# One graph-convolution layer's two weight products done as seven products of halves, moved between the two attention pairs

## The chip, the cores and the metric

The kernel runs on one core of one Trainium2 chip, in one launch, on inputs and outputs in float32. The metric is the device time of the launch in microseconds (us): the median of three runs.

## What is computed

There are 16 independent examples, each a table of 1024 nodes by 256 channels, and one table of neighbours `adj` (1024 by 1024) that all share. Each example goes through two layers. The first is an attention of 4 heads whose queries come from a weighted neighbour sum; the second is a pair of graph convolutions. Both add their input and normalize. Cut to what matters:

```
# layer 0
g   = relu(einsum('bcn,bnm->bcm', x^T, adj * likeness(x)) * para)      # queries
k,v = x @ kv_w
x1  = layernorm(x + softmax(q k^T * scale) v)
# layer 1
h1  = relu(x1 @ w1_loop + adj @ (x1 @ w1_neigh) + b1)                  # 256 -> 128 channels
h2  = relu(h1 @ w2_loop + adj @ (h1 @ w2_neigh) + b2)                  # 128 -> 256 channels
out = layernorm(x1 + (x1 + h2) * 0.5)
```

In the program the weights are named `w1n` (neigh) and `w1l` (loop). The change is about `x1 @ w1_neigh` (called t1), `x1 @ w1_loop` (the loop term), and the statistics of the last layernorm ("LN2").

## The kernel before

The kernel is a software pipeline over the examples, written out by hand: each engine executes its instructions in the order in which `run()` (from L1265) emits them, and an instruction waits until its inputs are there and its output buffer is free. While iteration `b` does the attention of example b, it also does the first convolution of example b-1 (`c1`), the second convolution of example b-2 (`c2`), the last normalization of example b-3 (`c3`), and the queries, keys and values of example b+1. Iterations 2 to 14 take the branch from L1398, and iteration 15 takes the one at L1442 and L1519; those fourteen are the ones that the change touches. The first two iterations and the end after iteration 15 have code of their own.

One iteration of the steady state is, in TensorE's order:

1. `both_units(0)` (L774): scores (L715) and weighted values (L761) of the first pair of heads. A pair has two units of 512 queries; a unit has eight score tiles of 128 keys. `scores` puts a tile in a PSUM tile called "big" (two banks, three such tiles exist), or, for every fourth, in two single banks; ScalarE takes the exponential into an SBUF row tile (L720, L722); VectorE adds the eight exponentials (L734, L736), turns the sum (L743) and reduces it (L749). `outputs` then reads the exponentials again, and each one's row tile comes free after that read.
2. `both_units(1)`: the same for the second pair.
3. `c1.inner()` (L910): t1 of example b-1. Sixteen products of 128 by 128 by 128 with channel-major x1 as the stationary operand, so that t1 comes out with nodes on partitions; ScalarE copies it out (L918).
4. `Joined.run` (L1204): the neighbour sums of t1 (for example b-1) and of h1 (for b-2) together, as seven products of halves (L1201) against stored parts of `adj`. The loop term is accumulated by `c1.loop` (L922) straight into the same PSUM banks: columns 0 to 511 ahead of product 1, columns 512 to 1023 ahead of product 3. The h2 products (L1026) lie inside it.
5. The queries (L660) and the keys and values (L448, L452) of example b+1.

"Seven products of halves" is the scheme in which a product of two by two blocks takes seven block products and some additions in place of eight. The kernel used it already for the queries, keys and values, the neighbour sums, and h2.

A float32 product of 128 by 128 by 512 is two matmul instructions here. The trace's counts are instructions.

SBUF work space is mostly one ring of 31 row tiles (`row_tile`, L99) of 128 by 1024 floats. A new row takes the slot that came free longest ago, and its first writer waits for that slot's last reader. All data transfers are issued on SyncE's queue (SPq), in program order; a transfer that waits for a row holds up those behind it. `before_convolution` (L1406) issues the first parts of `adj` for `Joined.run` and two rows of `adj` for the queries. It is emitted after the scores of the second pair.

`Joined.left` (L1187) makes sums of t1 and h1 on GpSimd (L1192 to L1195), and `q.left` sums of x (L619 to L622), which overwrite the blocked copy of x that `channel_major` (L1418) has turned.

The LN2 statistics are `c3.moments()` (L1422): eight times bn_stats (L314) and bn_aggr (L315) on VectorE, then eps (L319) and GpSimd's power (L320). `finish_aside` (L1075) applies them on ScalarE.

A row tile, the transposition by VectorE (which turns 32 by 32 blocks) and a write to DRAM with a permuting pattern turn a whole table: `turn_blocks` (L941) and `load_h1` (L950) do this for h1 already.

Of the kernel before, what the change touches and what calls it, by code (L numbers as in the profile page):

```python
# [18 lines left out]
def kernel(  # L19
# [34 lines left out]
    P = 128  # L54
# [33 lines left out]
    def half_psum(name):  # L88
        return big_psum(name)[:, 0:FB]
# [40 lines left out]
    kv_sums = dram.tile([P, N], F32, tag="kv_sums", name="kv_sums", bufs=1)  # L130
    w2_sums = dram.tile([P, 5 * P], F32, tag="w2_sums", name="w2_sums", bufs=1)

    def sum_kv_weights():
# [11 lines left out]
    def load_weights():  # L145
        nc.sync.dma_start(out=w1l_sb, in_=w1_loop.rearrange("(cc p) f -> p cc f", p=P))
        nc.sync.dma_start(out=w1n_sb, in_=w1_neigh.rearrange("(cc p) f -> p cc f", p=P))
        nc.sync.dma_start(out=w2l_sb, in_=w2_loop)
        nc.sync.dma_start(out=w2n_sb, in_=w2_neigh)
        nc.sync.dma_start(out=b1_sb, in_=b1.rearrange("(p o) -> p o", o=1))  # L150
        nc.sync.dma_start(out=b2_sb, in_=b2.rearrange("(o f) -> o f", o=1).to_broadcast([P, C]))

        for w in (w2l_sb, w2n_sb, b2_sb):
            nc.gpsimd.tensor_scalar_mul(w, w, 1.0 / 3.0)
        for w in (w1l_sb, w1n_sb):
            nc.gpsimd.tensor_scalar_mul(w, w, LIFT)
# [8 lines left out]
        nc.sync.dma_start(out=w2_sums, in_=t[:, 0:5 * P])  # L165

    ident = const.tile([P, P], F32, name="ident")
# [519 lines left out]
    class Attention:  # L687
# [85 lines left out]

        def both_units(self, pair, first=lambda: None, second=lambda: None, third=lambda: None):  # L774
            u = NJ * pair
# [11 lines left out]
            self.collect(u + 1, 6, 7)  # L787
            accB = self.turned_sum(u + 1)
            self.outputs(u + 1, turned=False)
            nc.vector.transpose(row[:, FB:N], self.o.pop(u + 1))  # L790
            self.part_sum(u + 1, accB)
            third()
# [106 lines left out]
    class GraphConv:  # L899


        def __init__(self, b, xT, nodes=None, x=None):
            self.b, self.xT, self.nodes, self.x = b, xT, nodes, x
            self.w2 = None

# [4 lines left out]
        def inner(self):  # L910
# [6 lines left out]
            self.t1 = row_tile(f"t1_{b}").rearrange("p (t f) -> p t f", f=HID)  # L917
            nc.scalar.copy(self.t1, p1.rearrange("p (t f) -> p t f", f=HID))  # L918

        def loop(self, ph, j, start=False, again=False):  # L920
# [147 lines left out]
        def deviation(self):  # L1068
            self.rstd = reciprocal_deviation(self.mv, f"g{self.b}", EPS2)

        def finish(self, dst):
            normalize(self.mv, self.rstd, self.x)
            nc.sync.dma_start(out=dst.rearrange("(t p) c -> p t c", p=P), in_=self.x)

        def finish_aside(self, dst, halfway=lambda: None):  # L1075

            shift = small.tile([P, NT], F32, tag="shift", name=f"shift_{self.b}", bufs=1)
            nc.vector.scalar_tensor_tensor(shift, self.mv[:, :, 0], -1.0, self.rstd, op0=ALU.mult, op1=ALU.mult)
            for t in range(NT):
# [6 lines left out]
        def ending(self, dst, quarters, aside, filled):  # L1086
# [18 lines left out]
            def deviations(*tiles):  # L1105
# [7 lines left out]
                statistics(mv, rows, range(n), f"e{tiles[0]}")  # L1113
                (nc.vector if tiles == (NT - 1,) else nc.gpsimd).tensor_scalar_add(rstd, mv[:, :, 1], EPS2)
                nc.gpsimd.tensor_tensor(rstd, rstd, neg_half[:, 0:n], ALU.pow)
# [13 lines left out]
            half = FB // NJ  # L1129
            banks = {}  # L1130
# [12 lines left out]
            aside(lambda: nc.scalar.copy(self.uT[:, FB:FB + half], third[:, 0:half]))  # L1143
            products(0, 1)
# [16 lines left out]
            leave(*stats)  # L1161
            products(6)
            stats = deviations(6)
            leave(*stats)
            products(7)
            _, mv, rstd, _ = deviations(7)
            normalize(mv, rstd, self.x[:, 7:8, :], 1)
            nc.sync.dma_start(out=dst[7 * P:8 * P, :], in_=self.x[:, 7, :])

    class Joined:  # L1170
# [33 lines left out]
        def run(self, between=None, last=None):  # L1204
# [18 lines left out]
            self.product(2, third)  # L1223
            nc.vector.tensor_add(p1, p1, third)
# [40 lines left out]
    def run():  # L1265
# [59 lines left out]
        for b in range(B):  # L1325
# [72 lines left out]
            elif more:  # L1398
                nodes = None

                def sums():
                    nonlocal nodes
                    nodes = NodeSums(q, xb, str(b + 1))
                    c2.load_x()

                def before_convolution():  # L1406
# [22 lines left out]
                def more_weights():  # L1429
# [3 lines left out]
                    if c3:  # L1433
# [6 lines left out]
                         last=nc.gpsimd)  # L1440
                c1.turn_blocks()
            else:  # L1442
                att.both_units(0)
                att.both_units(1, third=lambda: att.add_pairs(0))
# [74 lines left out]
            else:  # L1519
                c2.load_x()  # L1520
                both.fetch("00", "10", 2, 3)
                c1.inner()
                both.left(nc.gpsimd)
# [95 lines left out]
```

## Time and profile before

| | |
|---|---|
| median of 3 runs | 2119.41 us (2119.29 to 2120.25) |
| the profiled execution | 2119.75 us |
| its span, first to last instruction | 2118.0 us |
| granted TensorE clock | 0.999 |
| busy: TensorE, VectorE, ScalarE, GpSimd | 2107.8, 1866.3, 1136.3, 338.8 us |
| one steady iteration | 130.31 us |
| moved by DMA | 346.38 MB, mean 164 GB/s |

The period is the distance of the same instruction in two iterations (the first scores begin at 1172.74 and at 1303.05). In the profile PE is TensorE's matmul, PEld its weight load, DVE VectorE, ACT ScalarE, POOL GpSimd, SPq SyncE's DMA queue. A matmul's shown duration includes its way through the pipeline, so the pace is read from the chain of waits, which lists consecutive work with start, duration and number of instructions.

### The profile page before, as it was taken

Reading aid. Unit: us, or ns where it says so; the run is one execution under the profiler, and the core shown is the slowest. Engines: PE = TensorE matmul, PEld = TensorE weight load, DVE = VectorE, ACT = ScalarE, POOL = GpSimd, SP = SyncE. Lnnn points to the kernel's source line nnn. Section 1 sums busy time; section 2 is a strip of 40 time slices with the busy share of each in tenths; the row PEclk is TensorE's granted clock in tenths of the full one; section 3 lists DMA queues with packets and bytes.
Section 4 is the critical chain, followed back from the end, with each engine's and each line's share of the span. In section 5 each row is a group of like instructions: output and inputs, shape, how many; then the busy total and the mean of one; then the engine's idle time right before and its main releaser. Section 6 shows DMA issues by size and latency. Waiting matters only on the chain.

```text
span 2118.0 us, 24985 instructions
## 1 busy us (share of the span) xinstructions
PE 2107.8 (100%) x8724; PEld 1034.4 (49%) x8724; DVE 1866.3 (88%) x2264; ACT 1136.3 (54%) x1673; POOL 338.8 (16%) x223
## 2 busy tenths in 40 slices
PE   9999999999999999999999999999999999999998
PEld 5344435445454454545545454454544535445355
DVE  6899998898898998888988889888898888898875
ACT  5845564546546465473654736447455474555523
POOL 2010102131021311203122031210312102131022
PEclk9999999999999999999999999999999999999999
DMA  9495764856639476384764749557385673955545
GB/s 221 113 181 190 141 184 141 157 181 130 209 106 192 175 137 221 109 166 175 144 217 118 162 169 169 195 127 171 146 178 187 145 177 125 190 177 132 176 131 176
DMA packets 613732, 346.38 MB, mean 164 GB/s; under 512 B 492000, under 2 KB 556896, under 8 KB 613600
## 3 DMA queue, kind: packets, MB, share of 16 engines
q1 hardware_dynamic: 613328, 344.45, 63.0%
q8 instruction: 71, 1.16, 0.2%
q14 instruction: 61, 0.50, 0.1%
q10 hardware_dynamic: 272, 0.26, 0.0%
HBM read 294.45 MB, written 50.20 MB: 163 GB/s over the span
## 4 chain that ended last, share of the span: by engine, by line
PE 99%; DVE 0%; POOL 0%; issue 0%; POOLq 0%; DVEq 0%
PE s L715 21%; PE av L761 21%; PE hu_ps L1201 17%; PE g_ps L660 16%; PE v_ps L452 5%; PE k_ps L448 5%; PE hu_ps L1026 4%; PE t_ps L915 3%; PE g_ps L579 3%; PE hu_ps L922 2%; PE u_ps L966 1%; PE h_ps L937 1%; PE h_ps L1026 1%; PE sum_ps L275 0%; PE idle L1275 0%; PE h_ps L922 0%
## 5 line engine op out<-in xcount | busy, mean ns | idle before, releaser
L736 DVE TENSOR_TENSOR acc<-acc,pr 128x1024 f32<-128x1024 f32 x384 | 481.2, 1253 | 34.6 <-DVE acc L736 0.5
L722 ACT ACTIVATE pr<-s 128x1024 f32<-128x1024 f32 x392 | 391.5, 1121 | 173.9 <-PE s L715 173.9
L715 PE MATMUL s<-qT,kT 64*128 64x512 f32 x2048 | 448.7, 592 | 0.0
L761 PE MATMUL av<-pr,v 128*64 128x512 f32 x2048 | 447.0, 594 | 0.0
L715 PEld LDWEIGHTS s<-qT,kT 64*128 64x128 f32 x2048 | 195.3, 187 | 241.7 <-issue 183.7
L761 PEld LDWEIGHTS av<-pr,v 128*64 128x64 f32 x2048 | 144.1, 137 | 297.3 <-issue 269.1
L1201 PE MATMUL hu_ps<-adj,R 128*128 128x512 f32 x480 | 213.6, 592 | 0.0
L365 POOL TENSOR_TENSOR rstd<-rstd,neg_half 128x32 f32<-128x32 f32 x16 | 88.3, 5520 | 625.3 <-DVE rstd L363 625.3
L1192 POOL TENSOR_TENSOR R<-h 128x512 f32<-128x512 f32 x14 | 29.6, 2116 | 810.0 <-DVE o L786 697.2
L571 DVE SCALAR_TENSOR_TENSOR wg<-wg,adj 128x1024 f32<-128x1024 f32 x128 | 150.2, 1212 | 3.6 <-ACT wg L566 3.6
L720 ACT ACTIVATE pr<-s 128x512 f32<-128x512 f32 x240 | 143.0, 708 | 0.0
L565 ACT ACTIVATE wg<-c_row,c_sums 128x1024 f32<-128x1024 f32 x120 | 139.7, 1164 | 2.1 <-DVE wg L571 0.9
L1201 PEld LDWEIGHTS hu_ps<-adj,R 128*128 128x128 f32 x480 | 89.0, 190 | 100.9 <-issue 100.7
L566 ACT ACTIVATE wg<-wg 128x1024 f32<-128x1024 f32 x128 | 135.4, 1057 | 4.1
L918 ACT COPY t<-t_ps 128x1024 f32<-128x1024 f32 x16 | 16.2, 1014 | 174.9 <-PE t_ps L915 174.9
L660 PE MATMUL g_ps<-wg,x 128*128 128x512 f32 x224 | 107.7, 593 | 0.0
L660 PE MATMUL g_ps<-T,xB 128*128 128x512 f32 x208 | 107.3, 597 | 0.0
L660 PE MATMUL g_ps<-wg,xB 128*128 128x512 f32 x208 | 106.2, 592 | 0.0
L1201 PE MATMUL hu_ps<-adj,t 128*128 128x512 f32 x240 | 105.7, 592 | 0.0
L734 DVE TENSOR_TENSOR acc<-pr,pr 128x1024 f32<-128x1024 f32 x64 | 77.9, 1217 | 22.4 <-ACT pr L722 22.4
L743 DVE STREAM_TRANSPOSE accB<-acc 128x1024 f32<-128x1024 f32 x64 | 79.7, 1245 | 2.2
L749 DVE TENSOR_REDUCE den_part<-accB 128x32 f32<-128x1024 f32 x64 | 76.9, 1201 | 1.2
(252 smaller groups left out, 3070.7 us busy)
## 6 DMA issues: line engine op xcount, KB each, us to landing
adj<-adjT SPq DMA_DIRECT2D x210, 512.0 KB
adj<-in_adj_dram SPq DMA_DIRECT2D x128, 512.0 KB
para<-in_L_gnn_para_dram SPq DMA_DIRECT2D x32, 512.0 KB
xB_a<-in_x_dram SPq DMA_DIRECT2D x128, 128.0 KB
x1d<-xB_a SPq DMA_DIRECT2D x128, 128.0 KB
x<-x1d SPq DMA_DIRECT2D x16, 1024.0 KB
xB<-in_x_dram SPq DMA_DIRECT2D x120, 128.0 KB
x<-in_x_dram SPq DMA_DIRECT2D x15, 1024.0 KB
```

The costliest lines, as they stand in the source:

```text
L448: nc.tensor.matmul(dst, self.a[0][n], self.w[n], start=not again, stop=True, skip_group_check=again)
L452: nc.tensor.matmul(dst[:, ts(t, P)], self.w[n][:, ts(t, P)], self.a[1][n], start=not again and t == 0, stop=True, skip_group_check=again o ...
L565: nc.scalar.activation(wg, self.c_row, AF.Abs, bias=self.c_col[:, t:t + 1], scale=-1.0)
L566: nc.scalar.activation(wg, wg, AF.Tanh, scale=-0.5 / C)
L571: nc.vector.scalar_tensor_tensor(wg, wg, 1.0, self.adj.pop(t), op0=ALU.add, op1=ALU.mult)
L660: nc.tensor.matmul(self.p[n], x_n[:, k, :], w_n, start=(k == 0), stop=(k == TJ - 1))
L715: nc.tensor.matmul(halves[s], self.kT[rows, pair, ts(mt, P)], self.qT[rows, pair, ts(j, FB)], start=True, stop=True)
L720: nc.scalar.activation(pr[:, ts(s, FB)], halves[s], AF.Exp)
L722: nc.scalar.activation(pr, ps, AF.Exp)
L736: nc.vector.tensor_add(self.acc, self.acc, prs[mt])
L761: nc.tensor.matmul(pav[s * HD:(s + 1) * HD, :], self.v[:, mt, pair * P + s * HD:pair * P + (s + 1) * HD], prs[mt][:, ts(s, FB)], start=(mt ...
L1201: nc.tensor.matmul(dst, self.x[n][:, k, :], of_rows(rows, k), start=(start and k == 0), stop=(k == TJ - 1), skip_group_check=again)
```

## The change

`c1.inner()` and both `c1.loop` calls go for the fourteen examples of the steady state. `fast_inner`, called between the two attention pairs, computes the product of [w1n | w1l] with x1 by seven products of 128 by 128 by 512 with weights (or sums of weights, from DRAM) as stationary operand. The result is channel-major. The loop half stays in a row tile, `loops`; VectorE turns the t1 half, which goes through DRAM (`t1d`) and comes back with nodes on partitions. In `Joined.run` ScalarE copies one half of `loops` into the bank ahead of product 2, and VectorE adds the other half after product 3. The transposition of the next x moves from after the second pair into `fast_inner`. The reduction of unit u+1's exponential sum moves ahead of `outputs(u + 1)` in the first pair. The LN2 statistics become two passes on ScalarE (sum, then squares around the mean), an iteration apart. In the last example's `ending`, tile 5 changes its PSUM bank, and the last two tiles leave by VectorE.

```diff
+    w1_sums = dram.tile([P, 4 * P], F32, tag="w1_sums", name="w1_sums", bufs=1)
...
+        nc.gpsimd.tensor_add(s1, a21, a22)
+        nc.gpsimd.tensor_sub(s2, s1, a11)
+        nc.gpsimd.tensor_sub(s3, a11, a21)
+        nc.gpsimd.tensor_sub(s4, a12, s2)
+        nc.sync.dma_start(out=w1_sums, in_=t[:, 0:FB])
...
             accB = self.turned_sum(u + 1)
+            if summed:
+                self.part_sum(u + 1, accB)
+                summed()
             self.outputs(u + 1, turned=False)
             nc.vector.transpose(row[:, FB:N], self.o.pop(u + 1))
-            self.part_sum(u + 1, accB)
+            if not summed:
+                self.part_sum(u + 1, accB)
             third()
...
+        def load_inner(self):
+            self.w1 = row_tile(f"w1_sums_{self.b}")
+            nc.sync.dma_start(out=self.w1[:, 0:FB], in_=w1_sums)
+
+        def inner_sums(self):
+            w11, w12, w21, w22 = (self.xT[:, cc, ts(j, FB)] for cc in range(NC) for j in range(NJ))
+            t13, t24 = (row_tile(f"X_{self.b}_{k}") for k in range(2))
+            t1, t3, t2, t4 = t13[:, 0:FB], t13[:, FB:N], t24[:, 0:FB], t24[:, FB:N]
+            nc.vector.tensor_sub(t1, w12, w11)
+            nc.vector.tensor_sub(t2, w22, t1)
+            nc.vector.tensor_sub(t3, w22, w12)
+            nc.vector.tensor_sub(t4, w21, t2)
+            s1, s2, s3, s4 = (self.w1[:, ts(n, P)] for n in range(4))
+            self.inner_factors = {1: (w1n_sb[:, 0, :], w11), 2: (w1n_sb[:, 1, :], w21), 3: (s4, w22),
+                                  4: (w1l_sb[:, 1, :], t4), 5: (s1, t1), 6: (s2, t2), 7: (s3, t3)}
...
+        def fast_inner(self, aside=lambda: None):
...
+            upper, lower, chain = (half_psum(f"in_ps_{b}_{i}") for i in range(3))
+            s12, s34, t1T, self.loops, t1B = (row_tile(f"in_{b}_{i}") for i in range(5))
+            p1, u2, u3, p7 = s12[:, 0:FB], s12[:, FB:N], s34[:, 0:FB], s34[:, FB:N]
+            product(1, chain)
+            nc.scalar.copy(p1, chain)
+            product(2, upper)
+            nc.vector.tensor_add(t1T[:, 0:FB], p1, upper)
+            aside()
+            product(6, chain, again=True)
+            nc.scalar.copy(u2, chain)
+            product(7, lower)
+            nc.scalar.copy(p7, lower)
+            product(5, chain, again=True)
+            nc.scalar.copy(u3, chain)
+            nc.vector.tensor_add(self.loops[:, FB:N], u3, p7)
+            product(4, lower, again=True)
+            nc.vector.tensor_add(self.loops[:, 0:FB], u2, lower)
+            product(3, chain, again=True)
+            nc.scalar.copy(t1T[:, FB:N], chain)
+            nc.vector.transpose(t1B, t1T)
+            self.t1d = dram.tile([N, HID], F32, tag="t1d", name=f"t1d_{b}", bufs=2)
+            for a in range(Q):
+                nc.sync.dma_start(out=self.t1d[:, a * S:(a + 1) * S].rearrange("(bn k) r -> k bn r", k=S),
+                                  in_=by_node(t1B[a * S:(a + 1) * S, :]))
+
+        def load_t1(self):
+            self.t1 = row_tile(f"t1_{self.b}").rearrange("p (t f) -> p t f", f=HID)
+            nc.sync.dma_start(out=self.t1, in_=self.t1d.rearrange("(t p) f -> p t f", p=P))
...
+        def sums_aside(self):
+            self.mv = small.tile([P, NT, 2], F32, tag="mv", name=f"mv_{self.b}", bufs=2)
+            for t in range(NT):
+                nc.scalar.activation(self.x[:, t, :], self.x[:, t, :], AF.Identity, accum_out=self.mv[:, t, 0:1])
+
+        def squares_aside(self):
+            self.centred = True
+            nc.vector.tensor_scalar_mul(self.mv[:, :, 0], self.mv[:, :, 0], -1.0 / C)
+            scratch = work.tile([P, FB], F32, tag="o", name=f"squares_{self.b}")
+            for t in range(NT):
+                nc.scalar.activation(scratch[:, ts(t % 2, C)], self.x[:, t, :], AF.Square, bias=self.mv[:, t, 0:1],
+                                     accum_out=self.mv[:, t, 1:2])
+
+        def deviation_aside(self):
+            self.rstd = small.tile([P, NT], F32, tag="rstd", name=f"rstd_{self.b}", bufs=2)
+            nc.vector.tensor_scalar(self.rstd, self.mv[:, :, 1], 1.0 / C, EPS2, op0=ALU.mult, op1=ALU.add)
+            nc.gpsimd.tensor_tensor(self.rstd, self.rstd, neg_half[:, 0:NT], ALU.pow)
...
-            fourth = big_psum(f"u_ps_{self.b}_{NJ}")
+            fourth = half_psum(f"u_ps_{self.b}_{NJ}")
...
-            bias(fourth[:, FB:N], 5)
...
+            def copy_third():
+                nc.scalar.copy(self.uT[:, FB:FB + half], third[:, 0:half])
+                bias(third, 5)
...
-            products(6)
-            stats = deviations(6)
-            leave(*stats)
-            products(7)
-            _, mv, rstd, _ = deviations(7)
-            normalize(mv, rstd, self.x[:, 7:8, :], 1)
-            nc.sync.dma_start(out=dst[7 * P:8 * P, :], in_=self.x[:, 7, :])
+            for t in (6, 7):
+                products(t)
+                _, mv, rstd, _ = deviations(t)
+                last.append((t, mv, rstd))
+            for t, mv, rstd in last:
+                normalize(mv, rstd, self.x[:, t:t + 1, :], 1)
+                nc.sync.dma_start(out=dst[t * P:(t + 1) * P, :], in_=self.x[:, t, :])
...
-            c1.loop(third, 0, start=True)
+            if c1.loops is None:
+                c1.loop(third, 0, start=True)
+            else:
+                nc.scalar.copy(third, c1.loops[:, 0:FB])
...
-            c1.loop(first, 1, again=True)
+            if c1.loops is None:
+                c1.loop(first, 1, again=True)
...
-            c1.relu(1, first)
+            if c1.loops is None:
+                c1.relu(1, first)
+            else:
+                loop = c1.loops[:, FB:N]
+                nc.vector.tensor_add(loop, loop, first)
+                c1.relu(1, loop)
...
                 def sums():
                     nonlocal nodes
                     nodes = NodeSums(q, xb, str(b + 1))
+                    if c3:
+                        c3.squares_aside()
                     c2.load_x()
+                    c1.load_inner()
+
+                def summed():
+                    c1.inner_sums()
+                    if c3:
+                        c3.deviation_aside()
...
                 def before_convolution():
                     both.fetch("00", "10")
                     for t in (0, TJ):
                         q.load(t)
                         q.likeness(t)
                     both.fetch(2, 3)
-
-                att.both_units(0, sums, lambda: nodes.turn())
+                    c1.load_t1()
+
+                att.both_units(0, sums, lambda: nodes.turn(), summed=summed)
                 nodes.line()
                 nodes.row()
+                c1.fast_inner(turn_next)
                 att.both_units(1, before_convolution, third=lambda: (q.times_adj(0), q.times_adj(TJ)))
-                c1.inner()
-                xT_next = channel_major(blocked, f"xT_{b + 1}")
                 both.left(nc.gpsimd)
                 q.left(nc.gpsimd, blocked)
-                if c3:
-                    c3.moments()
...
                 c1.turn_blocks()
+                if b + 2 < B:
+                    c2.sums_aside()
             else:
-                att.both_units(0)
+                att.both_units(0, c1.load_inner, summed=c1.inner_sums)
+                c1.fast_inner()
                 att.both_units(1, third=lambda: att.add_pairs(0))
```

More of the change, by code (lines that the diff above doesn't have):

```diff
@@ L165, in load_weights @@
         nc.sync.dma_start(out=w2_sums, in_=t[:, 0:5 * P])
+        t = row_tile("w1_sums")
+        a11, a12, a21, a22 = (w[:, cc, :] for w in (w1n_sb, w1l_sb) for cc in range(NC))
+        s1, s2, s3, s4 = (t[:, ts(n, P)] for n in range(4))
+        nc.gpsimd.tensor_add(s1, a21, a22)
[3 more added lines that the diff above has]
+        nc.sync.dma_start(out=w1_sums, in_=t[:, 0:FB])
     ident = const.tile([P, P], F32, name="ident")
@@ L772, in turn, with both_units @@
             nc.vector.transpose(self.o[u], pav)
-        def both_units(self, pair, first=lambda: None, second=lambda: None, third=lambda: None):
+        def both_units(self, pair, first=lambda: None, second=lambda: None, third=lambda: None, summed=None):
             u = NJ * pair
@@ L903, in __init__ @@
             self.b, self.xT, self.nodes, self.x = b, xT, nodes, x
-            self.w2 = None
+            self.w2 = self.loops = None
+            self.centred = False
         def load_x(self):
@@ new lines, in fast_inner, with product @@
+        def fast_inner(self, aside=lambda: None):
+            b = self.b
+            def product(n, dst, again=False):
+                w, xs = self.inner_factors[n]
+                nc.tensor.matmul(dst, w, xs, start=not again, stop=True, skip_group_check=again)
+            upper, lower, chain = (half_psum(f"in_ps_{b}_{i}") for i in range(3))
[22 more added lines that the diff above has]
+                                  in_=by_node(t1B[a * S:(a + 1) * S, :]))
@@ L1077, in finish_aside @@
             shift = small.tile([P, NT], F32, tag="shift", name=f"shift_{self.b}", bufs=1)
-            nc.vector.scalar_tensor_tensor(shift, self.mv[:, :, 0], -1.0, self.rstd, op0=ALU.mult, op1=ALU.mult)
+            nc.vector.scalar_tensor_tensor(shift, self.mv[:, :, 0], 1.0 if self.centred else -1.0, self.rstd,
+                                           op0=ALU.mult, op1=ALU.mult)
             for t in range(NT):
@@ L1113, in deviations @@
                 statistics(mv, rows, range(n), f"e{tiles[0]}")
-                (nc.vector if tiles == (NT - 1,) else nc.gpsimd).tensor_scalar_add(rstd, mv[:, :, 1], EPS2)
+                (nc.vector if tiles[0] >= NT - 2 else nc.gpsimd).tensor_scalar_add(rstd, mv[:, :, 1], EPS2)
                 nc.gpsimd.tensor_tensor(rstd, rstd, neg_half[:, 0:n], ALU.pow)
@@ L1129, in ending @@
             half = FB // NJ
-            banks = {}
+            banks, last = {}, []
             self.uT = row_tile(f"uT_{self.b}")
             upper, third = (bank_psum(f"u_ps_{self.b}_{j}") for j in range(NJ))
-            fourth = big_psum(f"u_ps_{self.b}_{NJ}")
+            fourth = half_psum(f"u_ps_{self.b}_{NJ}")
             bias(filled[2], 6)
@@ L1142, in ending @@
             bias(upper, 0, 1)
-            aside(lambda: nc.scalar.copy(self.uT[:, FB:FB + half], third[:, 0:half]))
+            def copy_third():
+                nc.scalar.copy(self.uT[:, FB:FB + half], third[:, 0:half])
+                bias(third, 5)
+            aside(copy_third)
             products(0, 1)
@@ L1222, in run @@
             turn_to(1)
-            self.product(2, third)
+            self.product(2, third, again=c1.loops is not None)
             nc.vector.tensor_add(p1, p1, third)
@@ L1403, in sums, with turn_next @@
                     nodes = NodeSums(q, xb, str(b + 1))
+                    if c3:
+                        c3.squares_aside()
                     c2.load_x()
+                    c1.load_inner()
[3 more added lines that the diff above has]
+                        c3.deviation_aside()
+                def turn_next():
+                    nonlocal xT_next
+                    xT_next = channel_major(blocked, f"xT_{b + 1}")
+                xT_next = None
                 def before_convolution():
@@ L1521, in run @@
                 both.fetch("00", "10", 2, 3)
-                c1.inner()
+                c1.load_t1()
                 both.left(nc.gpsimd)
```

## The prediction

> **What bounds the kernel now.** First the page: busy time by engine, then the chain that ended last.
>
> ```profile
> span 2118.0 us, 24985 instructions
> ...
> PE 2107.8 (100%) x8724; PEld 1034.4 (49%) x8724; DVE 1866.3 (88%) x2264; ACT 1136.3 (54%) x1673; POOL 338.8 (16%) x223
> ...
> PE 99%; DVE 0%; POOL 0%; issue 0%; POOLq 0%; DVEq 0%
> ```
>
> TensorE is on the path for 99% of the span. Work taken from VectorE or ScalarE is worth nothing by itself; what counts is TensorE's instructions and every pause that the change puts between them. A busy share of 100% doesn't say that it runs at its pace, so next the chain in order of time, for one steady iteration (start, duration, line, instructions):
>
> ```profile
> 1172.74 13.93 PE s L715 x64
> 1186.68 13.88 PE av L761 x64
> 1200.56 13.94 PE s L715 x64
> 1214.49 13.88 PE av L761 x64
> 1228.38 3.77 PE t_ps L915 x32
> 1232.15 1.72 PE hu_ps L922 x4
> 1233.87 6.87 PE hu_ps L1201 x16
> ...
> 1254.69 1.72 PE hu_ps L922 x4
> ...
> 1259.91 2.82 PE hu_ps L1026 x24
> ...
> 1291.57 0.89 PE v_ps L452 x8
> ```
>
> Three prices come out of it. A matmul instruction over 512 columns paces at 6.87/16 = 0.4294 us, so a float32 product, two of them, costs 0.859. One over 128 columns paces at 0.89/8 = 0.111. And there are pauses: 64 score instructions, which run two at a time on half the rows, would take 32 x 0.4294 = 13.74 but take 13.93 (0.19 more); the values take 0.14 more; t_ps takes 3.77 where 32 x 0.111 = 3.56 (0.21 more). Each of these follows a change between half-array and whole-array matmuls. Then the other engines around the new place, 1200.5, from the timeline of VectorE,
>
> ```profile
> 1197.61 1.25 DVE L743 STREAM_TRANSPOSE accB<-acc 128x1024 f32<-128x1024 f32 x1
> 1200.61 0.72 DVE L790 STREAM_TRANSPOSE o<-av 128x512 f32<-128x512 f32 x1 [1.75 <-PE av L761]
> 1201.25 1.18 DVE L749 TENSOR_REDUCE den_part<-accB 128x32 f32<-128x1024 f32 x1
> ```
>
> and from that of SyncE's queue:
>
> ```profile
> 1215.40 0.33 SPq L549 DMA_DIRECT2D adj<-in_adj_dram  x1
> 1216.45 8.86 SPq L198 DMA_DIRECT2D adj<-adjT  x6
> ```
>
> VectorE is idle for 1.75 us before L790, and ScalarE for 9.69 before 1201.67. SyncE's loads come one by one as the values' matmuls (13.88/16 = 0.87 us per exponential tile) give back row tiles: rows, not bandwidth, set when they start.
>
> **What the Trainium skill says.** "TensorEngine Tiling (Array Packing)", Key Properties: changing the tiling mode drains TensorE. The trace agrees, at 0.14 to 0.21 us a change. "DMA: Bandwidth & Descriptors", Specifications: transfers under 512 B are not at line rate; the trace of before agrees (permuting 128 B writes of x1d and h1d run near 140 GB/s, plain adj loads near 400). The same page, Anatomy of one DMA, gives some 2.0 us fixed per DMA, on GpSimd's path; no run here shows it for SyncE apart, and I use 2.0 as an estimate for t1's load. "GPSIMD Engine Reference", Specifications: GpSimd shares SBUF interfaces with VectorE instructions that have two SBUF inputs; the trace agrees (L736 beside L1192 at 1222.37: 1.70 each in place of 1.25).
>
> **TensorE, part by part, per iteration.** Removed: 3.77 + 1.72 + 1.72 = 7.21. Added: 7 x 0.859 = 6.01. Mode changes: before, values to scores and values to t_ps; after, values to the seven products, products to scores, values to neighbour sums. That is one more; since t_ps's 3.77 held its own, two of 0.20 go onto the 6.01 (the scores' own stays in their row). Bounds 0.14 and 0.21 each.
>
> Waits inside `fast_inner`: `chain` is written, copied by ScalarE, and written again with one product between (6 after 1, 5 after 6, 3 after 5), and `lower` likewise (4 after 7). The nearest row is L1026, with the same pattern of copies (0.59 each): 2.82 where 24 x 0.111 = 2.67, so 0.15 for two waits, each under a cover of 0.89. The cover here is 0.86, so 0.03 more: about 0.11. I take 0.12 for 6, 5 and 3 and nothing for 4, whose cover the wait of 5 lengthens: 0.36. Bounds: 0.15 (three of 0.05, as in the k_ps pieces of 0.91 in place of 0.86) and 0.5.
>
> New stretch: 6.01 + 0.40 + 0.36 = 6.77. Gain 7.21 - 6.77 = 0.44 per iteration; fourteen iterations: 6.2 us.
>
> **What must stay hidden, and by what.**
> - `inner_sums`: four subtractions of about 0.64 (0.69 shown, overlapping), after the reduction L749 (1.18) that moves up: 1198.86 + 1.1 + 2.6 = 1202.6. Product 6 needs the second at about 1202.3; it is done at 1201.3. The 1.75 idle pays for it. L790 waits behind it, until 1203.3; its bank isn't asked for before 1208.
> - After it VectorE has the t1 sum (to 1203.9), the two transpositions of the next x (2.36, to 1206.2), the two loop sums (to 1207.5) and the turn of t1 (to 1209.1). Behind these stands the first sum of exponentials, ready no sooner than about 1210. The scores start at 1200.56 + 6.57 = 1207.1; their first tile takes `upper` (free 1203.9), their second, at 1208.0, `lower` (free when the last loop sum ends, 1207.6), the fourth `chain`. Margin 0.4: no stall taken, bounds 0 and 0.9.
> - ScalarE: five copies of 0.59 in its idle 9.69; the squares (8 x 0.4, the pace of L290) follow the L290 pass in the same gap. The sums (3.3) go between `finish_aside` and the squares of the first norm, which moves from 1277.9 to about 1281 or 1282; VectorE reads it at 1283.8. Nothing taken; 1 us later it would hold up the fold before the last query step.
> - VectorE loses the moments (120 x (0.395 + 0.182) in all; 4.9 an iteration) and gains 2.6 + 2.1 + 1.25 + 0.7: even, and no gain in time.
> - SyncE: the four t1d writes wait for VectorE until 1209 and take about 4 us to issue (as L947); `adj` parts 00 and 10 and two query loads stand behind them. They are wanted at 1235. GpSimd's eps and power (2.1) run while it is idle. `left` gets t1 earlier in its queue, so its sums move beside VectorE's last exponential sums; these have 6 us of slack.
> - t1's way back. `loops` holds one more row, so each load from `fetch(2, 3)` on comes one release later. t1's row is then the seventh of the third unit: 1214.49 + 6.57 + 7 x 0.87 + 0.15 = 1227.3. Four `adj` parts of 1.3 (0.52 MB at 400 GB/s) are ahead of it; with 2.0 for the data and 2.0 fixed it lands at 1232 to 1234. Wanted at 1228.38 + 6.57 = 1235. Nothing taken.
> - The weight sums at the start cost four small GpSimd steps and a store: hidden, TensorE has products to do.
>
> **The end.** Before, TensorE idles 0.65 for tile 5's bank, and the last tile waits for GpSimd's two steps of tile 6 (0.8 with their gaps). I take 0.4; bounds 0 and 1.
>
> **Sum.** 6.2 + 0.4 = 6.6. The profiled execution's 2119.75 (span 2118.0 and 1.75 around it) becomes 2113.1; the median stands 0.34 below it: **2112.8**.
>
> **Rivals.**
> - Copies nearly hidden, mode changes cheap: 7.21 - 6.01 - 0.28 - 0.15 = 0.77 per iteration, 10.8 + 0.9 at the end: 2107.7. For it: ScalarE has nothing else there. Against: L1026 does pause in the same pattern.
> - The second score tile waits for `lower`, behind x's transpositions on VectorE: 0.35 lost per iteration, 4.9 in all: 2117.7. For it: a margin of 0.4 on eight VectorE steps in a row. Against: the 1.75 idle ahead of them.
> - Slower: t1 lands after 1235 and product 1 stands still. Place: SyncE's queue behind row releases. Price: the lateness less the 0.44 gained, so it decides from 0.44 late; at 1.0 late 2119.4 + 14 x 0.56 - 0.4 = 2126.8. For it: a round trip in rows that are all taken, five transfers back to back. Against: 1 to 3 us of margin. That the scheme doesn't remove what it says is no case here: the matmul count falls by 26 an iteration (40 instructions out, 14 in).
>
> **How the numbers follow.** A measurement of this kernel can tell about 0.2% (4.2 us) from no change. Forecast 0.45, cheap copies 0.15, late `lower` 0.23, late t1 0.17. Faster by over 0.2% (under 2115.2): 0.42 + 0.15 + 0.04 = 0.61; within: 0.03 + 0.18 + 0.01 = 0.22; slower: 0.01 + 0.16 = 0.17. Range: from 2107.0 (cheap copies) to 2121.0 (the late `lower` at 0.6 an iteration), leaving out late t1 and the extremes.
>
> **What would show it.** In the chain after: the seven products as one stretch of 6.4 to 6.8 between values and scores; scores still 13.9; L1201 directly after the values, 0.2 longer in its first piece; a period of about 129.9. Wrong if a score piece grows (the `lower` rival: PEld L715 waiting for VectorE's loop sum), if PEld L1201 waits for a DMA of t1, or if the seven products take over 7.2.

## The result, and the profile after

| | before | after |
|---|---|---|
| median | 2119.59 us (4 runs) | 2149.43 us (4 runs, 2148.40 to 2150.09) |
| ratio | 1 | **1.0137**, 95% interval 1.0125 to 1.0150 |
| span of the profiled execution | 2118.0 us | 2148.3 us |
| granted TensorE clock | 0.999 | 0.995 |
| first score of example 0 | 48.45 | 65.83 |
| first score of example 2 | 260.41 | 279.67 |
| first score of example 3 | 390.71 | 412.38 |
| first score of example 15 | 1954.53 | 1982.50 |

The change made the kernel 1.4% slower; 2112.8 had been predicted. The page of the kernel after, the lines that answer to those of before (span; busy time; the chain's shares):

```profile
span 2148.3 us, 24753 instructions
...
PE 2108.7 (98%) x8360; PEld 994.1 (46%) x8360; DVE 1936.7 (90%) x2212; ACT 1254.9 (58%) x2126; POOL 371.1 (17%) x224
...
PE 8%; DVE 1%; issue 0%; ACT 0%; POOLq 0%; POOL 0%; DVEq 0%
```

Three things are to be read in them. 364 matmul instructions went (26 in each of 14 iterations, as the change says), and yet TensorE is busy 0.9 us longer. VectorE, which should have come out even, is busy 70 us longer for 52 instructions fewer: about half of that is that the new instructions are longer than the statistics that went (34 us by the prediction's own prices, see below), and the rest is that some instructions have become slower. And the chain is broken off: it accounts for a tenth of the span, so it can't be used here. What does the same service is the time at which each example's first score instruction starts, in TensorE's timeline (the last four rows of the table). Their differences put the 30.3 us of span in four places: **start**, up to example 2, +19.3; **example 2**, +2.4 (132.71 for 130.30); **twelve periods** from example 3 to 15, +6.3 (130.84 each for 130.32); **end**, +2.3 (165.8 for 163.5).

**The start.** ScalarE's timeline after:

```profile
28.66 1.06 ACT L575 ACTIVATE wg<-wg 128x1024 f32<-128x1024 f32 x1
52.59 1.15 ACT L574 ACTIVATE wg<-c_row,c_col 128x1024 f32<-128x1024 f32 x1 [22.88 <-DMA w_sums<-w_sums]
```

and TensorE's:

```profile
39.74 3.17 PE L588 MATMUL g_ps<-wg,x 128*128 128x512 f32 x7
56.20 5.60 PE L588 MATMUL g_ps<-wg,x 128*128 128x512 f32 x8 [13.29 <-DVE wg L580]
...
65.83 9.43 PE L724 MATMUL s<-qT,kT 64*128 64x512 f32 x34 [2.28 <-ACT qT L595]
```

The eighth likeness (L574) of the first queries stands 22.88 us and is released by a **store** to DRAM. The trace leaves the numbers out of names, so w1_sums and w2_sums look alike there; SyncE's queue tells them apart:

```profile
50.36 0.33 SPq L166 DMA_DIRECT2D w_sums<-w_sums  x1
52.13 0.33 SPq L174 DMA_DIRECT2D w_sums<-w_sums  x1
```

The releaser is L166, the store of the **w2** sums, which was there before the change: it is issued when GpSimd has made these sums, and the likeness starts 2.2 us later. For L174, the new store of the w1 sums, nobody waits. Nothing in a likeness reads w2_sums. A wait of a writer for a store of another tensor is a wait for a buffer: the row tag has 31 buffers (`ROWS`), the start fits into them before the change, and the tile of w1_sums is one more. So the ring is one slot further on when the eighth likeness asks: by this wait, it is given the row of the w2 sums, and stands until they have been stored. TensorE stands behind it for 13.29 us, and for 2.28 more later. After both pauses it crawls: the eight instructions at 56.20 take 5.60 (0.70 each; the seven ahead of the pause 3.17, 0.45 each).

**The iterations.** TensorE's timeline, example 9:

```profile
1225.06 1.98 PE L955 MATMUL in_ps<-x1T,w1n_sb 128*128 128x512 f32 x4
1226.88 2.91 PE L955 MATMUL in_ps<-X,w_sums 128*128 128x512 f32 x6
1229.62 1.03 PE L955 MATMUL in_ps<-X,w1l_sb 128*128 128x512 f32 x2
1230.48 1.10 PE L955 MATMUL in_ps<-x1T,w_sums 128*128 128x512 f32 x2
1231.52 14.00 PE L724 MATMUL s<-qT,kT 64*128 64x512 f32 x64
...
1260.11 3.24 PE L1290 MATMUL hu_ps<-adj,t 128*128 128x512 f32 x7 [0.70 <-PE av L770]
```

The seven products run as one stretch, from 1225.06 to 1231.52: 6.46. The new stretch is not what lost time. Product 1 is: it starts 1.30 after the start of the last values instruction, where an uninterrupted one follows after 0.52. The label in brackets names the values, but GpSimd's L1282, which reads t1 too, starts at 1260.15 with "DMA t<-t1d" as releaser: t1 has just landed. In other iterations the pause is elsewhere. The waits over examples 4 to 14 (engine, line, waited for: us in all, times, longest):

```profile
PEld hu_ps L1092 <- DVE uT L1334: 14.5, 11, 1.8
...
PE hu_ps L1092 <- DVE uT L1334: 6.2, 9, 1.0
...
PE hu_ps L1290 <- DMA t<-t1d: 1.8, 3, 0.9
```

The first product with w2n waits for uT (the neighbour sums of h1, which it reads) in nine of eleven. The same list of the kernel before has no wait of TensorE for uT or for a DMA of t1. Why uT is late shows in VectorE's timeline, example 8 (values end at 1128.76):

```profile
1130.55 3.83 DVE L580 SCALAR_TENSOR_TENSOR wg<-wg,adj 128x1024 f32<-128x1024 f32 x2
1134.30 1.76 DVE L641 TENSOR_TENSOR T<-wg 128x512 f32<-128x512 f32 x1
1136.09 1.65 DVE L642 TENSOR_TENSOR wg<-wg,wg 128x512 f32<-128x512 f32 x1
1137.66 1.76 DVE L643 TENSOR_TENSOR T<-wg,T 128x512 f32<-128x512 f32 x1
1139.62 1.47 DVE L644 TENSOR_TENSOR T<-wg,T 128x512 f32<-128x512 f32 x1 [0.20 <-PE hu_ps L1290]
...
1151.36 0.69 DVE L1334 TENSOR_TENSOR uT<-snap,hu_ps 128x512 f32<-128x512 f32 x1
```

The four sums L641 to L644 (the "T sums") take 0.69 each when they run alone, the two products of likeness and adjacency, L580, 2.35 together. Here they take 6.64 and 3.83, while seven of GpSimd's eight sums run from 1128.6 to 1140.5, at the very same time:

```profile
1131.04 2.26 POOL L1284 TENSOR_TENSOR R<-t,R 128x512 f32<-128x512 f32 x1
```

That the one slows the other is tested in experiments 5 and 6. In the kernel before, GpSimd's sums (1233.3 to 1243.0 there) lay mostly beside VectorE's transposition of x and the eight pairs of LN2 statistics, and neither side was slowed:

```profile
1235.23 0.39 DVE L314 BATCH_NORM_STATS2 st_g<-x 128x6 f32<-128x256 f32 x1
1235.79 1.27 POOL L1195 TENSOR_TENSOR R<-t,R 128x512 f32<-128x512 f32 x1
```

Only GpSimd's last two met T sums there (L633 and L634, 1.65 and 1.75). The change took the transposition and the statistics away from this place.

### The profile page after: what moved, and what is told of

Read it like the earlier page. It is cut to its first block, busy times and chain, and to the rows that moved or that the text cites. A ratio compares the mean times of both kernels' runs of the same rounds, so it can differ in the third digit from the quotient of the medians.

```text
span 2148.3 us, 24753 instructions
## 1 busy us (share of the span) xinstructions
PE 2108.7 (98%) x8360; PEld 994.1 (46%) x8360; DVE 1936.7 (90%) x2212; ACT 1254.9 (58%) x2126; POOL 371.1 (17%) x224
## 5 line engine op out<-in xcount | busy, mean ns | idle before, releaser
L580 DVE SCALAR_TENSOR_TENSOR wg<-wg,adj 128x1024 f32<-128x1024 f32 x128 | 170.9, 1373 | 26.7 <-ACT wg L575 26.6
L574 ACT ACTIVATE wg<-c_row,c_sums 128x1024 f32<-128x1024 f32 x120 | 139.4, 1162 | 18.9 <-DVE wg L580 17.3
L1313 ACT COPY snap<-hu_ps 128x512 f32<-128x512 f32 x15 | 8.8, 586 | 160.6 <-PE hu_ps L1290 160.6
L1153 POOL TENSOR_TENSOR rstd<-rstd,neg_half 128x8 f32<-128x8 f32 x12 | 19.6, 1638 | 472.6 <-DVE rstd L1152 472.6
L1281 POOL TENSOR_TENSOR R<-h 128x512 f32<-128x512 f32 x14 | 20.6, 1472 | 422.5 <-PE av L770 321.2
```

Of the source, the lines that this page charges most:

```text
L574: nc.scalar.activation(wg, self.c_row, AF.Abs, bias=self.c_col[:, t:t + 1], scale=-1.0)
L580: nc.vector.scalar_tensor_tensor(wg, wg, 1.0, self.adj.pop(t), op0=ALU.add, op1=ALU.mult)
```

## The experiments

Theory: three causes. One row tile too many, a 32nd, delays the start; t1's load is queued behind two adjacency parts and lands late; GpSimd's sums, started by t1, run beside VectorE's two-input instructions and delay uT. Rivals: the extra weights are what delays the start; the removed loop product was the cover that uT lacks; the statistics on ScalarE gain nothing. All kernels of this section but two start from the changed kernel with the shared row; a line dropped from the code makes its line numbers lower by one.

| kernel | median, us | ratio to before (95%) | examples 3 to 15, period |
|---|---|---|---|
| shared row | 2130.78 | 1.0048 (1.0034 to 1.0062) | 130.82 |
| kernel before, one row more | 2137.10 | 1.0079 (1.0065 to 1.0092) | 130.31 |
| shared row, t1 first | **2117.82** | **0.9988 (0.9981 to 0.9995)** | 129.92 |
| changed kernel, t1 first | 2136.03 | 1.0071 (1.0058 to 1.0085) | 129.94 |
| shared row, x sums after | 2151.68 | 1.0149 (1.0135 to 1.0163) | 132.35 |
| shared row, x sums first | 2121.58 | 1.0007 (0.9999 to 1.0015) | 130.02 |
| t1 first, x sums first | 2118.45 | 0.9990 (0.9982 to 0.9999) | 129.87 |
| shared row, more cover | 2131.33 | 1.0052 (1.0038 to 1.0066) | 130.84 |
| t1 first, statistics on VectorE | 2132.20 | 1.0056 (1.0042 to 1.0070) | 131.15 |
| t1 first, two small moves | 2119.89 | 1.0000 (0.9991 to 1.0008) | 129.97 |

**1. The shared row.** GpSimd writes the w1 sums over the w2 sums, once these are stored:

```diff
-        t = row_tile("w1_sums")
```

> The changed kernel, with the sums of w1n and w1l written into the row tile that the sums of w2n and w2l already have, so that the start uses 31 row tiles instead of 32. Theory one (the 32nd row): the last likeness of the start waits for the store of the w1 sums only because it is given their row; the wait of 22.9 us on ScalarE ends and the first scores start some 17 us earlier, near 48.5 us instead of 65.8; the time is near 2130 us (ratio to the kernel before 1.005). Theory two (the weights themselves): the start is later because eight weight tiles instead of six are loaded and GpSimd has four more sums to make; the same pause moves to another reader of them and the time stays near 2148 us (1.0135). Theory three (the whole loss sits in the iterations, the start only shifts a wait): also near 2148.

2130.78. ScalarE's timeline of this kernel has the eighth likeness right behind the seventh:

```profile
30.05 1.13 ACT L573 ACTIVATE wg<-c_row,c_col 128x1024 f32<-128x1024 f32 x1
```

The first score is at 48.45, to the hundredth where it was before the change. All weights and both sets of sums are still there, and even a new wait of 2.2 us on GpSimd for the first store. Theory one holds, and two and three fall: 18.7 us hung on one buffer.

**2. The row alone, in the kernel before.**

```diff
         nc.sync.dma_start(out=w2_sums, in_=t[:, 0:5 * P])
+        t = row_tile("one_more")
+        nc.gpsimd.tensor_sub(t[:, 0:P], b12, b11)
+        nc.sync.dma_start(out=one_more, in_=t[:, 0:P])
```

> The kernel before, with one row tile more at the start and nothing else of the change: GpSimd makes one subtraction of two w2 blocks more into it and SyncE stores it to a DRAM tile that nobody reads. Theory one (the 32nd row): the start of the kernel before grows by some 15 to 18 us, to about 2136 (ratio 1.0075), with the wait of the last likeness for that store in ScalarE's waits. Theory two (the weights): one small subtraction and a store of 64 KB are nothing, 2119.5 (1.000).

```profile
50.54 1.15 ACT L570 ACTIVATE wg<-c_row,c_col 128x1024 f32<-128x1024 f32 x1 [20.15 <-DMA w_sums<-w_sums]
```

2137.10, 16.9 us more, with the same wait at the same place, and for the same store: that of the w2 sums is issued at 48.25 and the likeness starts 2.3 later; for the store of the new row, issued at 48.67, nobody waits. The cause is shown in both directions. Its periods are 130.31, those of before.

**3. t1 first.**

```diff
                     both.fetch("00", "10")
+                    c1.load_t1()
                     for t in (0, TJ):
                         q.load(t)
                         q.likeness(t)
                     both.fetch(2, 3)
-                    c1.load_t1()
```

> The kernel of the run with the shared row, with the load of t1 put on SyncE's queue ahead of the coordinates and of two adjacency parts (after the first two parts). Theory one (t1 behind the parts): t1 lands some 2 us earlier, product 1 waits no more for it (0.2 to 1.1 us in half of the iterations), but uT on VectorE is late then: the two pauses stand in for each other, so the time is within 3 us of the run with the shared row. Rival: the two add up, and 4 to 6 us go.

2117.82: 13.0 us less than with the shared row, more than either theory gave, and 2.4 less than the kernel before in the same series (2120.22). In the change as it stood, t1 was issued 54.5 us after the example's first score (1251.76), in this kernel 47.9 after (1220.09, with the score at 1172.16); product 1 wants it at 62.1. Both pauses go, not only product 1's. Of all waits of TensorE for uT over examples 4 to 14 this is left:

```profile
PEld hu_ps L1091 <- DVE uT L1333: 0.3, 1, 0.3
```

An early t1 starts GpSimd's sums early: L1281 runs at 1230.7, ahead of the end of values at 1234.2, and its last sum ends at 1242.6, 8.4 after that end (in example 8 of the change: 11.8 after). So fewer of them meet VectorE's products. The expectation that the two pauses would stand in for each other failed: both hang on when t1 lands.

**4. Do the two causes add up?** The same move in the changed kernel, with the 32nd row.

> The changed kernel as it stands (the w1 sums in a row tile of their own), with t1's load put on SyncE's queue ahead of the coordinates and two adjacency parts. If the late start and the late t1 are two causes that add up, the early t1 gives here what it gave with the shared row, 13 us: 2149.4 - 13.0 = 2136.4. If the late start upsets the later stages too, or the early t1 only helped because of it, another number: under 2132 or over 2141.

2136.03, within 0.4 us of the sum. The losses of the start and of the iterations add up.

**5. GpSimd's x sums after the joined products.**

```diff
-                q.left(nc.gpsimd, blocked)
                 kv = KeysValues(b + 1, xT_next)
...
                          last=nc.gpsimd)
+                q.left(nc.gpsimd, blocked)
```

> The kernel of the run with the shared row, with the four sums of x that GpSimd makes for the next batch's first Strassen products moved from ahead of the joined products to after them, so that GpSimd works on them 13 us later and not beside VectorE's products of likeness and adjacency. Theory one (GpSimd beside VectorE slows it): the products on VectorE take 2.35 us for two again instead of 3.52 and the T sums 0.69 each, uT is made some 3 us earlier, the wait of the first product with w2n for uT (0.5 to 1.1 us in about half of the iterations) goes; t1's wait ahead of product 1 stays or takes its place: 3 to 6 us less than with the shared row alone if it does not take its place, 0 to 2 less if it does. Theory two (the removed loop product was all of the cover; GpSimd is nothing): within 1 us of the run with the shared row.

2151.68: 20.9 us **more**. Both theories missed it. The four sums still take 6.3 us, and now they lie beside another chain of two-input sums. VectorE's timeline of this kernel after uT:

```profile
1271.36 0.69 DVE L1333 TENSOR_TENSOR uT<-snap,hu_ps 128x512 f32<-128x512 f32 x1 [3.35 <-PE hu_ps L1289]
...
1272.95 1.64 DVE L1081 TENSOR_TENSOR last<-h1T,last 128x512 f32<-128x512 f32 x1
1274.52 1.76 DVE L1082 TENSOR_TENSOR last<-uT 128x512 f32<-128x512 f32 x1
```

The first line confirms theory one's half: uT is early (VectorE waits 3.35 for TensorE). The others show the price: L1081 and L1082 take 1.64 and 1.76 for 0.69, L579 behind them 3.42 for 2.35, and the second half of the last products waits for VectorE's L1113, 13.8 us in ten of eleven iterations.

**6. GpSimd's x sums first.**

```diff
-                both.left(nc.gpsimd)
                 q.left(nc.gpsimd, blocked)
+                both.left(nc.gpsimd)
```

> The kernel of the run with the shared row, with GpSimd's four sums of x put ahead of its four sums of t1 and h1. The first of the eight, as the code stands, waits some 5 us for t1; in this order it does not. Theory one (GpSimd's sums beside VectorE's products make uT late): the x sums run before t1 lands, so that fewer are left beside the products, but t1's own sums end 5 us later and product 5 or 6 may wait; uT pauses go, t1's stay: some 2122 to 2128. Theory two (the order of the sums does not matter, only t1's time): within 2 us of 2130.8.

2121.58, 9.2 us less than the shared row, by an exchange of two lines. The work is the same; four of the eight sums now run before t1 lands. VectorE's timeline of this kernel, example 8:

```profile
1110.12 0.69 DVE L641 TENSOR_TENSOR wg<-wg,wg 128x512 f32<-128x512 f32 x1
...
1125.12 0.69 DVE L1333 TENSOR_TENSOR uT<-snap,hu_ps 128x512 f32<-128x512 f32 x1 [3.55 <-PE hu_ps L1289]
```

The sums take 0.69 again, and VectorE now waits 3.55 us for TensorE where TensorE waited for it. No wait for uT is left; those for t1 stay (1.3 us in four iterations, 1.3 more in two under the name of the values). Theory one holds, 0.4 us below the range that it gave: GpSimd beside VectorE made uT late, and a change of GpSimd's order alone undoes that, while t1 stays late.

**7. Both moves.**

> The kernel with the shared row and the early t1, with GpSimd's four sums of x ahead of its sums of t1 and h1. Each of the two moves took away 9 to 13 us alone. If they remove the same pause (t1 late, GpSimd's sums then beside VectorE's products, uT late), the second adds nothing to the first: 2117.8 within 1.5 us. If they remove two different pauses, 3 us or more come off: 2115 or less.

2118.45, the same as t1 first alone within 0.6 us: both moves remove the same pause of uT, and the early t1 removes its own besides.

**8. More cover.**

```diff
-            self.product(3, first, again=True, steps=range(0, TJ // 2))
+            self.product(3, first, again=True, steps=range(0, 3))
             rest = c2.last_products(third, second)
-            self.product(3, first, again=True, steps=range(TJ // 2, TJ))
+            self.product(3, first, again=True, steps=range(3, TJ))
```

> The kernel of the run with the shared row, with the four steps of product 3 that frame the last products split three ahead and one after instead of two and two: 0.86 us more of TensorE work stand between product 4 and the first product with w2n, which waits for uT. Theory one (uT is late for want of cover): the pauses ahead of the first product with w2n (0.9 us beyond the usual 0.43, in nine of the twelve full iterations of the shared-row run) go; those of product 1 ahead of t1 (0.3 to 1.2 us in six) stay or come in the iterations that had none, as the two have stood in for each other so far: between 2122 and 2128. Theory two (t1's lateness is the root and the uT pause only shows where the delay is paid): the pause goes from uT and comes back whole at t1, 2130 as with the shared row.

2131.33: nothing gained. The PE line for uT is gone from the list of waits, and the one for t1 has grown:

```profile
PE hu_ps L1289 <- DMA t<-t1d: 3.1, 6, 0.9
```

Theory two has the time right, and the place only in part. Where the time went, against the shared row, can be summed from the starts of TensorE's matmuls over examples 3 to 14. Some 7.7 us of pauses for uT went. At t1 only 0.8 came back (4.8 in all now, in eight of the twelve iterations and by up to 1.1). 4.3 came back in pieces of 0.1 to 0.2 an iteration at the second half of the last products, which now has one step of product 3 as cover in place of two, and at the query products behind it; and 2.6 ahead of the products with the sums of the keys' weights, which wait for a load. So more cover in one place did not pay, partly because it was taken from another; that t1 is the root rests on experiment 3, not on this one.

**9. The statistics back on VectorE**, with t1 first: `c3.moments()` after `q.left`, no `squares_aside`, `deviation_aside` or `sums_aside`.

> The kernel with the shared row and the early t1, with the LN2 statistics put back on VectorE (eight pairs of statistics instructions, 4.9 us in each full iteration, ahead of the joined products) and off ScalarE. Theory one (VectorE is the second bound between the end of values and uT, where it waited 1.5 us for TensorE with the early t1): uT is some 3 us late in each of twelve iterations, about 2150. Theory two (moving the statistics was not needed, VectorE has time): 2118.

2132.20, 14.4 us more than without: moving the statistics was needed, at 1.2 us an iteration, but not 2.7 as theory one had it. Between the products and the T sums VectorE now has 4.4 us of statistics, and

```profile
989.66 0.69 DVE L640 TENSOR_TENSOR T<-wg 128x512 f32<-128x512 f32 x1
```

the T sums are at 0.69 again: the statistics, 0.40 and 0.18 each, run beside the last of GpSimd's sums unslowed and shield what follows. From VectorE's transposition after the values to uT it takes 22.88 us here and 26.36 in the kernel before, which has the statistics (4.3) and the transposition of x (2.4) there. The change took these 6.7 away and should have come to 19.7: with t1 first it does (19.55, its wait of 1.51 for TensorE left out), but in example 8 of the change it is 22.55. The collision took back 2.8 more than in those two kernels, which have two slowed T sums each.

**10. Two small moves on top of t1 first:** in example 2 the sums of x1 ahead of VectorE's last exponential sums; in the last example the LN1 mean one product later.

> The kernel with the shared row and the early t1, with two small moves: in the third batch VectorE makes the four sums of x1 before its last exponential sums, not after them (TensorE waited 1.35 us for them there), and in the last batch the mean of the LN1 comes one product later (TensorE waited 0.4 us for its sums). If these pauses are on the path, 1 to 2 us less than the early t1 alone: 2116. If something else takes their place: 2118.

2119.89: no gain, and 2.1 us more than t1 first alone. Example 2 takes 131.48 for 131.52: its pause of 1.4 us has only moved, from the seven products to the scores behind them, which wait for the last loop sum (L972). VectorE is full there: busy for 4.93 of the 5 us from 290. The last example is longer, from its first score to the end 167.05 for 164.90:

```profile
2033.69 0.38 PE L283 MATMUL sum_ps<-sq_part,fold 128*128 128x32 f32 x2 [1.88 <-DVE sq_part L287]
```

The mean, made one product later, makes its squares later, and TensorE now waits for these. No kernel here is clearly faster than the one with t1 first.

## Why the prediction was wrong, step by step

- **"The weight sums at the start cost four small GpSimd steps and a store: hidden, TensorE has products to do."** The failed step, 18.7 of the 36.6 us between forecast and measurement. I counted the time of the added instructions, which was indeed hidden, and not the buffer that they take from the ring: one row more at the start, and the eighth likeness got the row of the w2 sums and waited 22.88 us for their store. Another 13.0 us were t1's late landing and what it set off (the third and fourth points below); the remaining 5 are mostly example 2 and the end. The prediction itself said, of SyncE's loads, that "rows, not bandwidth, set when they start", and counted one more row in `loops`; it didn't count the rows of the start.
- **TensorE's arithmetic held.** Forecast for the seven products 6.01 + 0.40 + 0.36 = 6.77 and a gain of 0.44 an iteration. Measured 6.46, and 0.19 more in the first piece of the neighbour sums (7.06 for 6.87), which the 6.77 contain: 6.65. The three waits between products were 0.08 each in place of 0.12. With t1 first this gave a period of 129.92 for 130.32, a gain of 0.40 (0.53 in an iteration free of other pauses: 1172.16 to 1301.93). A forecast of 129.9 for the period would have been right, but for the next two points.
- **"t1 ... lands at 1232 to 1234. Wanted at ... 1235. Nothing taken."** The issue time was right (1227.3 forecast, 54.6 after the example's first score; 1251.76 measured, 54.5 after). The landing was not: forecast 4.7 to 6.7 after the issue, measured 8.4 (1260.15). I had given the parts ahead of it 400 GB/s; while they moved, from 1248 to 1256, the transfers ran at

```profile
DMA packets 648, 2.40 MB, mean 300 GB/s; under 512 B 65, under 2 KB 65, under 8 KB 647
```

  300 GB/s. The trace of before could have warned of it: 326 GB/s from 1216 to 1224. This is the rival "t1 late", to which I gave 0.17. It named rightly that product 1 would stand still; but the lateness came from the transfers and not from row releases, and its price was taken as the lateness alone.
- **"its sums move beside VectorE's last exponential sums; these have 6 us of slack."** The step that made it dear. They moved beside the likeness products and T sums, 0 to 12 us after the values, where VectorE has no slack before uT. The prediction quoted the shared interface and a slowed L736, and then costed the meeting at nothing.
- **"VectorE loses the moments 4.9, gains 2.6 + 2.1 + 1.25 + 0.7: even".** Its own numbers say 6.65 more in fourteen iterations and 4.9 less in twelve, 34 us in all; VectorE's busy time rose by 70. The rest is mostly the collision (the likeness products alone went from 150.2 to 170.9 us, L571 and L580): the statistics had been the harmless neighbour of GpSimd's sums (experiment 9).
- **The end.** 0.4 gained was forecast. With t1 first it is 164.9 for 163.5, 1.4 lost: VectorE's LN1 chain in the last example holds TensorE, and in `ending` a product now waits 0.8 us for ScalarE's copy of uT (L1245), a wait that before has not. Example 2 loses 1.2 in the same kernel. Experiment 10 did not remove these; how to is open.
- **The "late `lower`" rival** did not occur: scores start 0.52 after the start of the last product instruction in example 9 (1231.52), the distance that a change of mode has elsewhere (values to product 1, uninterrupted: 0.52).

## What to carry over

When a step is added, count the buffers that it takes from a rotating pool at that moment, not only its instructions: with one tile over the pool's size, an unrelated writer was given a row still in use and waited for that row's last reader, here an old store, 22.9 us. When work leaves an engine, ask what it stood beside: VectorE instructions with one input were the shield against GpSimd's sums, and the two-input ones that took their place lost some 3 us to them. And when several pauses trade places from one iteration to the next, look for the transfer or queue that starts them all; covering one pause gained nothing, and an earlier load took away both.

## What the runs showed of the hardware

- **GpSimd beside VectorE.** "SBUF — State Buffer", section "SBUF: two separate sides", says that a VectorE instruction with two SBUF inputs and a GpSimd instruction take one pair of ports in turns, each for its whole length. The runs agree that both sides are slowed: a 0.69 us sum takes 1.65 to 1.76 beside GpSimd sums, which take 1.6 to 2.26 in place of 1.26; the one-input statistics stay at 0.40. I had not expected the order of two GpSimd calls to be worth 9.2 us of 2120.
- **TensorE after a pause.** Example 0's first 34 scores after the pause of 2.28 take 9.43 us; before, 36 took 8.00. With the 13.29 pause ahead of it this adds some 2 us twice to the start. "TensorE: Matmul & The Clock Gate", section "Part 1: The HAM clock gate", says that an idle array falls to half rate and needs some 3.4 us of work to come back. The trace agrees: the granted clock is 0.50 from 48 to 60 us, 1.00 from 62 to 66, 0.50 again from 68 to 70, and 1.00 from 72 on; in the kernel before it is 1.00 throughout these stretches. So the second pause, of only 2.28 us, was followed by a slow stretch of its own.
